# A decoder layer on one core: the first loads of the second stage in another order, and the cast of one bias row moved to an earlier step

## The chip, the core and the metric

The kernel runs on one core of one Trainium2 chip. The metric is the device time of one execution in microseconds (us), as the median of several runs. Five engines work side by side, each through its own list of instructions in order: TensorE (PE, the matmuls), VectorE (DVE), ScalarE (ACT), GpSimd (POOL) and SyncE (SP), which here does nothing but issue transfers (DMAs). ACT issues some transfers as well.

## The reference, cut to what matters

One decoder layer in three blocks, each with a residual and a layer norm behind it; x is 8 x 512 x 512, the context 8 x 512 x 1024, all float32.

```
x1 = layernorm(x  + self_attention(x))            # relative positions, over the axis of 8
x2 = layernorm(x1 + cross_attention(context, x1)) # 8 heads of 64
   # k, v = split(context @ W_src.T + b_src) * mask;  q = (x1 @ W_tgt.T + b_tgt) * mask
   # out  = concat(x1, softmax(q k / 8, masked) v) @ W_out.T + b_out
y  = layernorm(x2 + ffn(x2))
   # h = relu(x2 @ w1.T + b1) rounded to fp8;  w2 rounded to fp8, b2 rounded to fp16
   # ffn = round16(h @ w2.T + b2)
```

## The kernel before, in words

The work falls into two stages. **Stage one** does the self attention for all rows and projects the context of all eight batches to keys (kd) and values (vd), which it stores to device memory together with x1 (x1d). A scheduler orders it. Its last piece is the context of batch 6: `project_context` makes four key tiles (psk, L158) and four value tiles (psv, L172) on TensorE. ScalarE evicts each and issues its store (L167 and L181) right behind the eviction. The context of batch 7 is left for the second stage (the tiles ct7a and ct7b).

**Stage two** does cross attention and feed forward for the batches t = 0 to 7 under a manual schedule: on PE, DVE, ACT and SP the instructions stand in the order in which the Python code emits them. `weave` mixes two lists: the "dense" steps (projections, hidden layer) and the attention steps (`scores`, `attend_next`). `run` executes a step and, ahead of it, spends a credit of 0.7 of the step's cost on the list `side` (softmax work in small pieces, each with a cost) and calls `move`.

The steps that matter around the change, for batch t, head pair c and query half jj:

- `load` (L726) fetches a mask row (mbc). `load_x1T` (L755) fetches x1 of a batch as four transfers into x1Ts, and `turn_x1` (L759) transposes its 32 x 32 blocks on DVE (L753). `queries` (L822) multiplies x1Ts by w_tgt (psq, L825), and DVE evicts to qT (L832).
- `scores` (L836) makes the score tiles s (L845, two in PSUM at a time). DVE takes each out and finds its extreme (pe and nmax, L860), ACT takes the exponential (L870), DVE divides (L885) and transposes blocks into pb (L897).
- `move_blocks` (L902) copies pb to pT in 16 transfers on SP (L910). There is one pT buffer, so the 16 for head pair c can begin only when the `attend` of c - 1 (av, L945) has been done.
- `load_v` (L778) fetches the values of a head pair into the one buffer raw, in four transfers (L788). `turn_v` (L793) transposes them on DVE into vx (L799), and POOL multiplies by the mask (L803). `attend` needs both pT and vx.
- `later` holds loads that are due after some further calls of `move` (a count, taken down by one in each call, run when it falls below zero). `moves` holds the block moves, and in each call of `move` they go ahead of what `later` holds.
- `stage` and `convert` (L1085 and L1090) fetch w2 in four quarters (w2f) and cast each on DVE to fp8 (L1091). `cast_b2` (L1097) fetches the row b2 to all partitions (b2f, L1099) and casts it to fp16 (b2q, L1100). b2f takes one of the seven buffers with the tag "pe" in the pool sp, which the softmax tiles pe and the context tiles kst and vst share.

In the first round (t = 0) the dense steps are six of the eight tiles of batch 7's context (psk, psv) and the queries of batch 1. The dictionary `behind` hangs the casts on these steps by number.

The SP list at the head of the second stage is, in order: w_src (two halves), w_tgt, w_xo, then the output bias row bxo (L93, called from L719), x1Ts in four transfers, w2f, kT twice, raw in four, the next mask row, ct7a and ct7b, x1Ts of batch 1, and x1 of batch 0. In the built program bxo lies where the first context tile of batch 6 was, and so waits for TensorE to have read that tile for the last time.

Each transfer of SP or ACT uses one of eight counters in turn (as the built program lists them), and first waits until the transfer that used this counter before has landed.

Of the kernel before, what the change touches and what calls it, by code (L numbers as in the profile page):

```python
# [9 lines left out]
F32 = mybir.dt.float32  # L10
# [7 lines left out]
P = 128  # L18
E = 512
# [19 lines left out]
R_BQ, R_RW, R_BO, R_BXO, R_B2 = range(5)  # L39
# [3 lines left out]
def decoder_layer(  # L43
# [22 lines left out]
    nc = tc.nc  # L66

    def chunked(w):
        return w.rearrange("(c p) o -> p c o", p=P)
# [21 lines left out]
    def load_row(pool, r, name):  # L91
        tl = pool.tile([P, E], F32, name=name)
        nc.sync.dma_start(tl, rows[r].partition_broadcast(P))  # L93
        return tl
# [92 lines left out]
    with ExitStack() as ph:  # L187
# [439 lines left out]
        t = T - 2  # L627
# [29 lines left out]
    with ExitStack() as ph:  # L657

        def pool(name, bufs, **kw):
            return ph.enter_context(  # L660
                tc.tile_pool(name=name, bufs=bufs, reuse_waits="tile", **kw)
            )

        wb = pool("wb", 1)
# [3 lines left out]
        sp = pool("sp", 7)  # L668
# [10 lines left out]
        urgent, side = [], []  # L679
# [11 lines left out]
        moves, later = [], []  # L691
# [24 lines left out]
        x1Ts = wb.tile([P, 2, EC, S], F32, name="x1Ts")  # L716
        w_xo = wb.tile([P, 2 * EC, E], F32, name="w_xo")
        nc.sync.dma_start(w_xo, chunked(w_xoT))
        bxo = load_row(wb, R_BXO, "bxo")  # L719
        w2q = wb.tile([P, HC, E], F8, name="w2q")  # L720
        b2q = wb.tile([P, E], F16, name="b2q")

# [22 lines left out]
        def load_blocks(dst, src):  # L745
            for a in range(4):
                nc.sync.dma_start(
                    dst[32 * a : 32 * a + 32].rearrange("p c (m e) -> p c m e", e=32),
                    src.rearrange("j (g r) (c a e) -> a r c (j g) e", r=32, a=4, e=32)[a],
                )  # L750

        def turn_in_place(dst, c):
            nc.vector.transpose(dst[:, c], dst[:, c])  # L753

        def load_x1T(t):  # L755
            x1T[t] = x1Ts[:, t % 2]
            load_blocks(x1T[t], x1d[t])

        def turn_x1(t):  # L759
            for c in range(EC):  # L760
                turn_in_place(x1T[t], c)
# [16 lines left out]
        def load_v(p):  # L778
            t, c = p // EC, p % EC
            if p >= T * EC:  # L780
                return
            if t >= T - 2:
                v[t, c] = kvd.tile([P, ST, P], F32, tag="v", name=f"vx{t}_{c}")
                nc.sync.dma_start(v[t, c], vd[t][:, :, c * P : (c + 1) * P])
                return
            raw[p] = kvd.tile([P, 4, P], F32, tag="raw", bufs=1, name=f"raw{p}")
            for g in range(4):
                nc.sync.dma_start(  # L788
                    raw[p][32 * g : 32 * g + 32],
                    vd[t][:, c, g * P : (g + 1) * P].rearrange("(b r) q -> r b q", r=32),  # L790
                )

        def turn_v(p):  # L793

            t, c = p // EC, p % EC
            v[t, c] = kvd.tile([P, ST, P], F32, tag="v", name=f"vx{t}_{c}")
            nc.vector.transpose(  # L799
                v[t, c].rearrange("p s (b e) -> p b s e", e=32),  # L800
                raw[p].rearrange("p b (s e) -> p b s e", e=32),
            )
            nc.gpsimd.tensor_tensor(  # L803
                v[t, c],
                v[t, c],
                maskcol[:, t, :].unsqueeze(2).to_broadcast([P, ST, P]),
                ALU.mult,
            )
            if p + 1 < (T - 2) * EC:
                later.append([2, lambda: load_v(p + 1)])  # L810

        def turn_v_soon(p):
            if p < (T - 2) * EC:
# [271 lines left out]
        def stage(q):  # L1085

            w2f.append(qx.tile([P, HC // 4, E], F32, tag="hq", name=f"w2f{q}"))
            nc.sync.dma_start(w2f[q], chunked(w2T)[:, q * 4 : q * 4 + 4, :])
# [6 lines left out]
                stage(q + 1)  # L1095

        def cast_b2():  # L1097
            b2f = sp.tile([P, E], F32, tag="pe", name="b2f")
            nc.sync.dma_start(b2f, rows[R_B2].partition_broadcast(P))  # L1099
            side.append((("b2", 0), 0.5, lambda: nc.vector.tensor_copy(b2q, b2f)))  # L1100

        def of(cost, f, *a):
            return [(cost, lambda: f(*a))]
# [63 lines left out]
        with tc.manual_schedule(engines={ET.PE, ET.DVE, ET.Activation, ET.SP}):  # L1167
            mq = load(0)
            load_x1T(0)
            stage(0)  # L1170
            for c in range(2):
                load_k(0, c)
            load_v(0)
            turn_x1(0)
            for o in range(EC):
                queries(0, o, mq)
            scores(*units[0])
            turn_v_soon(0)

            for t in range(T):  # L1180
                dense = []
                projected = 0
                mq = load(t + 1) if t + 1 < T else None
                asked = [of(3.6, queries, t + 1, o, mq) for o in range(EC) if t + 1 < T]
                asked = sum(asked, [])
                if t == 0:

                    ct = [
                        qx.tile([P, FC // 2, S], F32, tag="x2T", name="ct7a"),
                        qx.tile([P, FC // 2, S], F32, tag="x1", bufs=2, name="ct7b"),  # L1190
                    ]
                    for i in range(2):
                        nc.sync.dma_start(
                            ct[i],
                            chunked(ctxT[T - 1])[:, i * (FC // 2) : (i + 1) * (FC // 2), :],
                        )
                    load_x1T(1)
                    load_x1(0)
                    pieces = project_context(
                        T - 1,  # L1200
                        w_src[:, :, 0:E],
                        w_src[:, :, E:],
                        lambda f: ct[f // (FC // 2)][:, f % (FC // 2), :],
                        ps_b,
                        "b",
                        sp,
                        "pe",
                    )
                    steps = sum([of(7.2, piece) for piece in pieces[:-2]], []) + asked

                    behind = {
                        1: of(0.0, convert, 0),
                        3: of(0.0, convert, 1),
                        4: of(0.0, turn_x1, 1),
                        5: of(0.0, convert, 2) + of(0.0, cast_b2),
                        7: of(0.0, convert, 3),
                    }
                    for i, step in enumerate(steps):
                        dense += [step] + behind.get(i, [])
                    queried = len(dense)  # L1220
                else:
                    done = [of(3.8, finish, t - 2, j, NJ) for j in range(NJ) if t > 1]
                    if t == 1:

                        done = [of(7.2, pieces[-2]), of(7.2, pieces[-1]), [], []]
                    dense += output_of(t - 1)
                    projected = len(dense)

                    if t + 1 < T:
                        dense += of(0.0, load_x1T, t + 1)  # L1230
                    dense += done[0] + of(0.0, normalize_x2, t - 1)
                    dense += done[1] + of(0.0, load_x2T, t - 1)
                    if t == 1:
                        dense += of(0.0, load_w1)
                    dense += done[2]
                    if t + 1 < T:
                        dense += of(0.0, turn_x1, t + 1)
                    dense += done[3]
                    dense += asked[:2] + of(0.0, turn_x2, t - 1) + asked[2:]
                    queried = len(dense)  # L1240
                    for n in range(HC):
                        dense += of(3.6, hidden, t - 1, n)
                        if n == HC // 4:
                            dense += of(0.0, load_x1, t)
                weave(dense, attention_of(t, projected, queried))

            last = of(3.8, finish, T - 2, 0, NJ) + output_of(T - 1)
            last += of(0.0, normalize_x2, T - 1)
            for j in (1, 2):
                last += of(3.8, finish, T - 2, j, NJ)  # L1250
            for j in range(NJ):
                last += of(0.6, turn_last_x2, j)
            last += of(3.8, finish, T - 2, 3, NJ)
            for n in range(HC):
                last += of(3.6, hidden, T - 1, n)
            for j in range(NJ):
                last += of(3.8, finish, T - 1, j, 1)
            for cost, step in last:
                run(cost, step)
            settle(("y", T - 1))  # L1260
# [88 lines left out]
```

## Time and profile before

| what | value |
|---|---|
| median of 3 runs | 2140.01 us (2139.88 to 2142.92) |
| the profiled execution's own time | 2137.83 us |
| its span in the trace | 2136.0 us |
| busy: PE, DVE, ACT, POOL | 2059.9, 1435.1, 467.5, 172.1 us |
| mean granted TensorE clock | 0.989 |
| PE idle, 890 to 1116 us, by waits | 7.9, 9.0, 0.4, 6.1, 4.5, 1.2 and 0.7 us |

Times in the views are counted from the start of the span. A line of the timeline gives the start, the duration, the engine and line, the operation with the tiles it writes and reads, the number of instructions merged, and in brackets the idle time ahead of it with what ended it. SPq and ACTq are the transfers issued by these engines; their duration is that of issuing, not of the transfer. The table of windows gives the busy time of each engine in each stretch, with the granted TensorE clock (1.00 is full).

### The profile page before, as it was taken

Reading aid. Unit: us, or ns where it says so; the run is one execution under the profiler, and the core shown is the slowest. Engines: PE = TensorE matmul, PEld = TensorE weight load, DVE = VectorE, ACT = ScalarE, POOL = GpSimd, SP = SyncE. Lnnn points to the kernel's source line nnn. Section 1 sums busy time; section 2 is a strip of 40 time slices with the busy share of each in tenths; the row PEclk is TensorE's granted clock in tenths of the full one; section 3 lists DMA queues with packets and bytes.
Section 4 is the critical chain, followed back from the end, with each engine's and each line's share of the span. In section 5 each row is a group of like instructions: output and inputs, shape, how many; then the busy total and the mean of one; then the engine's idle time right before and its main releaser. Section 6 shows DMA issues by size and latency. Waiting matters only on the chain.

```text
span 2136.0 us, 17269 instructions
## 1 busy us (share of the span) xinstructions
PE 2059.9 (96%) x5768; PEld 881.0 (41%) x5768; DVE 1435.1 (67%) x2285; ACT 467.5 (22%) x955; POOL 172.1 (8%) x147
## 2 busy tenths in 40 slices
PE   9899999999999999897999999999999999999998
PEld 5444444444444444342334443444444434443443
DVE  4999999999999994076454664845747648356332
ACT  3011102101200111122133232332332332323211
POOL 0201010110012010010101011010010100000000
PEclk9999999999999999998899999999999999999999
DMA  6511430454015355675484653745647538436200
GB/s 213 202 44 44 183 114 20 153 190 166 13 55 202 118 187 179 157 186 133 99 204 117 111 136 78 140 109 98 133 100 113 133 85 148 101 72 150 57 20 20
DMA packets 246201, 255.27 MB, mean 120 GB/s; under 512 B 141024, under 2 KB 161504, under 8 KB 246112
## 3 DMA queue, kind: packets, MB, share of 16 engines
q1 hardware_dynamic: 228736, 223.45, 41.3%
q10 hardware_dynamic: 17376, 30.71, 4.0%
q8 instruction: 46, 0.75, 0.1%
q14 instruction: 43, 0.35, 0.1%
HBM read 130.36 MB, written 56.62 MB: 88 GB/s over the span
## 4 chain that ended last, share of the span: by engine, by line
PE 67%; DVE 22%; DMA 5%; issue 3%; SPq 2%; POOL 1%; ACT 1%; ACTq 0%; DVEq 0%; POOLq 0%
PE h L1037 20%; PE pox L982 5%; PE av L945 5%; PE s L845 5%; PE psq L825 5%; PE pox L970 5%; PE o L1054 4%; DVE pq L388 4%; DVE sc L397 4%; DVE pv L437 4%; PE px L553 3%; DVE pv L447 2%; PE psk L158 2%; PE ps_q L212 2%; PE psv L172 2%
## 5 line engine op out<-in xcount | busy, mean ns | idle before, releaser
L1037 PE MATMUL h<-x2T,w 128*128 128x512 f32 x1024 | 454.2, 599 | 4.8 <-DVE x2T L753 4.8
L1037 PEld LDWEIGHTS h<-x2T,w 128*128 128x128 f32 x1024 | 192.0, 191 | 263.4 <-issue 255.6
L860 DVE CUSTOM_DVE_ANT_0 pe<-s,mb 128x512 f32<-128x512 f32 x256 | 162.1, 681 | 204.4 <-PE s L845 204.4
L870 ACT ACTIVATE pe<-pe,nmax 128x512 f32<-128x512 f32 x256 | 182.2, 712 | 234.0 <-DVE nmax L860 231.7
L897 DVE STREAM_TRANSPOSE pb<-pe 128x512 f32<-128x512 f32 x256 | 159.6, 679 | 0.0
L1044 ACT ACTIVATE hq<-h,colv 128x512 fp8e4<-128x512 f32 x128 | 88.0, 687 | 294.3 <-PE h L1037 294.3
L437 DVE TENSOR_TENSOR pv<-v,sc 128x2048 f32<-128x2048 f32 x64 | 149.6, 2338 | 2.0
L388 DVE TENSOR_TENSOR pq<-qw,k 128x2048 f32<-128x2048 f32 x64 | 148.3, 2317 | 1.2
L397 DVE TENSOR_REDUCE sc<-pq 128x64 f32<-128x2048 f32 x64 | 146.0, 2281 | 1.3
L845 PE MATMUL s<-kT,qTx 64*128 64x512 f32 x512 | 129.5, 623 | 9.5 <-DVE nmax L860 9.4
L945 PE MATMUL av<-pT,vx 128*64 128x512 f32 x512 | 121.6, 619 | 11.3 <-DMA pT<-pb 6.1
L212 PE MATMUL ps_q<-w_in,xt 128*128 128x512 f32 x256 | 119.7, 597 | 6.3 <-DVE qw L374 6.3
L825 PE MATMUL psq<-x1Ts,w_tgt 128*128 128x512 f32 x256 | 115.4, 603 | 9.1 <-DVE x1Ts L753 9.1
L212 PE MATMUL ps_k<-w_in,xt 128*128 128x512 f32 x256 | 115.5, 601 | 5.3 <-DMA xt<-in_xT_dram 4.9
L463 PE MATMUL po<-w_o,aoT 128*128 128x512 f32 x256 | 119.1, 608 | 0.7 <-ACT aoT L460 0.7
L885 DVE TENSOR_SCALAR pe<-pe,rden 128x512 f32<-128x512 f32 x256 | 116.4, 497 | 4.5
L982 PE MATMUL pox<-w_xo,uT 128*128 128x512 f32 x256 | 115.2, 598 | 0.0
L970 PE MATMUL pox<-w_xo,x1Ts 128*128 128x512 f32 x256 | 114.4, 595 | 0.0
L1054 PE MATMUL o<-w2q,hq 128*128 128x512 fp8e4 x512 | 114.1, 379 | 0.0
L212 PE MATMUL ps_v<-w_in,xt 128*128 128x512 f32 x256 | 112.0, 594 | 0.0
L473 POOL TENSOR_TENSOR r<-r,bo 128x512 f32<-128x512 f32 x32 | 55.6, 1763 | 507.5 <-DMA r<-in_x_dram 438.8
L989 DVE TENSOR_TENSOR x<-pox,x 128x512 f32<-128x512 f32 x32 | 22.1, 692 | 104.7 <-PE pox L982 66.7
(142 smaller groups left out, 2163.2 us busy)
## 6 DMA issues: line engine op xcount, KB each, us to landing
pT<-pb SPq DMA_DIRECT2D x512, 128.0 KB, 2.4
ch<-in_ctxT_dram SPq DMA_DIRECT2D x24, 512.0 KB, 5.9
td<-tx SPq DMA_DIRECT2D x12, 768.0 KB, 5.9
tx<-td SPq DMA_DIRECT2D x12, 768.0 KB, 7.9
r<-in_x_dram SPq DMA_DIRECT2D x32, 256.0 KB, 3.6
x1d<-r ACTq DMA_DIRECT2D x32, 256.0 KB, 2.5
x1Ts<-x1d SPq DMA_DIRECT2D x32, 256.0 KB, 6.2
kT<-kd SPq DMA_DIRECT2D x32, 256.0 KB, 3.2
```

The costliest lines, as they stand in the source:

```text
L212: nc.tensor.matmul(ps, lhsT=xt[:, e, :], rhs=w_in[:, e, part * E : (part + 1) * E], start=(e == 0), stop=(e == EC - 1),)
L388: nc.vector.tensor_tensor(pr, qw[:, fs] .rearrange("p (h d) -> p h d", d=D1) .unsqueeze(2) .to_broadcast([P, HH, T, D1]), k_all[:, :, fs]. ...
L397: nc.vector.tensor_reduce(sc[:, t, g * HH * T : (g + 1) * HH * T], pr.rearrange("p h s d -> p (h s) d"), AX.X, ALU.add,)
L437: nc.vector.tensor_tensor(pr, v_all[:, :, fs].rearrange("p s (h d) -> p s h d", d=D1), sc[:, t, g * HH * T : (g + 1) * HH * T] .rearrange( ...
L825: nc.tensor.matmul(ps, lhsT=w_tgt[:, e, o * P : (o + 1) * P], rhs=x1T[t][:, e, :], start=(e == 0), stop=(e == EC - 1),)
L845: nc.tensor.matmul(ps[:, h, :], lhsT=qT[t][half[h], c, j * P : (j + 1) * P], rhs=kT[t, c][half[h], :], start=True, stop=True,)
L870: nc.scalar.activation(pe, pe, AF.Exp, bias=nmax[:, h : h + 1], scale=-1.0, accum_out=den[:, h : h + 1],)
L945: nc.tensor.matmul(av[half[h], :], lhsT=v[t, c][:, s, half[h]], rhs=pT[t, c][:, :, :, s, h].rearrange("p g i q -> p (g i) q"), start=(s == 0),
L970: nc.tensor.matmul(po, lhsT=x1T[t][:, e, j * P : (j + 1) * P], rhs=w_xo[:, e, :], start=(e == 0), stop=False,)
L982: nc.tensor.matmul(po, lhsT=uT[t][:, e, j * P : (j + 1) * P], rhs=w_xo[:, EC + e, :], start=False, stop=(e == EC - 1),)
L1037: nc.tensor.matmul(ps, lhsT=w1[0][:, e, n * P : (n + 1) * P], rhs=x2T[t][:, e, :], start=(e == 0), stop=(e == EC - 1),)
L1054: nc.tensor.matmul(po, lhsT=hq[t][:, c, j * P : (j + 1) * P], rhs=w2q[:, c, :], start=(c == 0), stop=(c == HC - 1),)
```

## The change

Four edits, all of which act in the first round of the second stage:

- The load of bxo is issued behind the four transfers of x1Ts for batch 0 instead of ahead of them.
- The load of b2f is issued behind the first raw load, with the first loads of the stage, instead of behind the third quarter of w2.
- The cast to b2q stands behind the first quarter's cast, as a step of its own, instead of in the list `side` behind the third quarter.
- In batch 0 the load of the next raw is due in the next call of `move` (count 0) instead of two calls later (count 2).

```diff
@@ ahead of the stage
         nc.sync.dma_start(w_xo, chunked(w_xoT))
-        bxo = load_row(wb, R_BXO, "bxo")
         w2q = wb.tile([P, HC, E], F8, name="w2q")
@@ turn_v(p)
             if p + 1 < (T - 2) * EC:
-                later.append([2, lambda: load_v(p + 1)])
+                later.append([2 if t else 0, lambda: load_v(p + 1)])
@@ cast_b2()
         def cast_b2():
-            b2f = sp.tile([P, E], F32, tag="pe", name="b2f")
-            nc.sync.dma_start(b2f, rows[R_B2].partition_broadcast(P))
-            side.append((("b2", 0), 0.5, lambda: nc.vector.tensor_copy(b2q, b2f)))
+            nc.vector.tensor_copy(b2q, b2f)
@@ the manual schedule
             load_x1T(0)
+            bxo = load_row(wb, R_BXO, "bxo")
             stage(0)
             for c in range(2):
                 load_k(0, c)
             load_v(0)
+            b2f = sp.tile([P, E], F32, tag="pe", name="b2f")
+            nc.sync.dma_start(b2f, rows[R_B2].partition_broadcast(P))
@@ behind, t == 0
-                        1: of(0.0, convert, 0),
+                        1: of(0.0, convert, 0) + of(0.0, cast_b2),
...
-                        5: of(0.0, convert, 2) + of(0.0, cast_b2),
+                        5: of(0.0, convert, 2),
```

## The prediction

> **What bounds the kernel now.** I read the page's part 1 and its slices first, then the waits of TensorE between 820 and 1120 us, then, for each long wait, the chain and the timelines of SP and DVE around it. PE is busy for 96% of the span and idle in few places. So a change pays only where it closes an idle stretch of PE, or the slow clock behind one.
>
> ```profile
> PE 2059.9 (96%) x5768; PEld 881.0 (41%) x5768; DVE 1435.1 (67%) x2285; ACT 467.5 (22%) x955; POOL 172.1 (8%) x147
> PEclk9999999999999999998899999999999999999999
> ```
>
> The clock dips in two slices alone, from about 960 to 1070 us. The waits of PE around there (total, times, longest):
>
> ```profile
> PE s L845 <- DVE nmax L860: 9.4, 2, 9.0
> PE psq L825 <- DVE x1Ts L753: 9.1, 2, 7.9
> PE av L945 <- DMA pT<-pb: 6.1, 1, 6.1
> PE av L945 <- POOL vx L803: 4.5, 1, 4.5
> ```
>
> Four stalls; behind them PE runs until 1936 us with under 2 us of waiting. The chain shows what feeds three of them. At the head of the stage:
>
> ```profile
> 864.01 21.47 PE psv L172 x50
> ...
> 885.50 0.34 SPq L93
> ...
> 891.69 6.83 DMA x1Ts<-x1d
> ...
> 898.64 0.72 DVE x1Ts L753
> ```
>
> SP stood at bxo (L93) until TensorE had read the first context tile for the last time. x1Ts was queued behind it, and its last piece landed at 898.5. PE ran out at 891.47 and went on at 899.41. In the middle:
>
> ```profile
> 983.56 5.66 DMA b2f<-in_rows_dram
> ...
> 989.24 0.43 DVE b2q L1100
> 989.67 0.60 DVE pe L860
> ...
> 990.95 3.79 PE s L845 x8
> ```
>
> DVE stood at the cast of b2 until its row landed, with the score evictions (L860) queued behind it. PE, done at 981.94, waited for these until 990.95. And at the end of the round, on SP:
>
> ```profile
> 1020.07 11.30 SPq L910 DMA_DIRECT2D pT<-pb  x16
> 1031.47 1.95 SPq L788 DMA_DIRECT2D raw<-vd  x4
> ```
>
> The values of the last head pair go out behind 16 moves. They land at 1035.1, are turned and masked, and av starts at 1037.19 where PE was free at 1032.65.
>
> **Part 1: x1 ahead of bxo.** Nothing is added; five transfers change places on SP. In the built program's list of waits the four x1Ts pieces now wait for the landing of four ACT stores alone, two of keys and two of values (issued at 857.90, 864.76, 871.63 and 878.50; such stores land in 2.4 us, one in 6.9). So the last piece goes out at about 881. Issue (0.7) and landing (4.3, the least of the x1Ts rows, to 6.8, the row above) bring it to 886 to 888.5, and the first turn (0.72) to 889.2 at the latest. That is 2.3 us before PE ends psv. The stall of 7.94 goes.
>
> What is passed: bxo waits for a later context tile and goes out at about 888.8. w2f keeps its own wait for the last psv (891.47) and kT its wait for the last value store (894.7 by the row), so these move by 2 us or less. bxo's reader, POOL at 925, keeps over 20 us of cover.
>
> The clock behind the stall: the four psq groups took 15.46 us (899.41 to the first s at 914.87). Two groups at full clock take 7.07 (1083.54 to 1090.61), so four take 14.14; 1.3 was lost. Sum: 7.94 + 1.3 = **9.2**, less whatever is late next. That is ct7a, needed at 891.47 + 14.14 + 1.95 (scores) = 907.6, and ct7b 3.5 later. Before they landed at 910.6 and 913.8 (issued 905.01 and 905.63, landing 5.6 and 8.2). They stood behind w2f, which shared the transfers with 1 MB of x1Ts and took 11.3 us; the other three w2f took 5.4 to 6.4. With x1Ts out of the way w2f lands at about 897.5 and kT at 899. ct7a goes out at about 900, with four raw and two row transfers ahead of it on SP, and lands at 905.6. Bounds of the wait: 0 (this reckoning) to 3.0 (ct7 no earlier than before). I take 0.
>
> **Part 2: b2.** One transfer moves ahead of the mask row (0.35 us of SP, behind raw). One cast of 0.43 us moves on DVE to behind the first w2 cast, where DVE has a wait of 4.07 us for ACT a little later: nothing. In the old place DVE leaves the turn of the values at 982.65 + 0.70 = 983.35 and starts L860 there, not at 989.59: **6.2** earlier. PE's stall shrinks from 9.0 to 2.8; the rest is PE's own last psq, its eviction, the turn and the first L860. What is late next on DVE: the cast of w2's last quarter follows these four L860, and w2f is issued behind 16 moves as before, so DVE will wait for it some 3 us. Behind it stand divides and the eviction of the next psq, for which DVE has waits of 3.17 and 2.25 us on PE now, so this costs PE nothing. b2f holds one of seven buffers for longer. The list of waits shows one new wait from that: ACT's eviction kst (941.92) needs the first kst's store (issued at 924.68), which has 17.2 us for a landing of 2.4 to 6.9.
>
> The clock is the open size. The 2.8 us that stay have a nearest row, a gap of 2.88 us in stage one (columns as in the table of windows; PE busy first, clock third from the right):
>
> ```profile
> 608.96:612.37 3.41, 1.18 (x5) 0.48 (x5) 3.41 (x5) 0.59 (x1) 3.30 (x3) 1.00 0.00 0
> 612.37:615.78 3.41, 3.41 (x5) 1.51 (x5) 3.41 (x3) 0.00 (x0) 0.00 (x0) 0.50 0.00 0
> 981.01:984.43 3.42, 0.93 (x3) 0.10 (x1) 1.37 (x2) 0.00 (x0) 1.00 (x1) 1.00 0.89 200
> ```
>
> Eight matmuls took 5.39 us behind it, against 3.6 elsewhere. So the clock can still fall to a half. Before, the score pair behind the stall took 3.71 (990.95 to 994.66) against 1.92, of which 0.35 is its second L860: 1.4 to 1.5 lost, which I leave lost, by that row. [...]
>
> **Part 3: raw ahead of the moves.** raw is one buffer, free once DVE has turned the pair before. That turn is at 1011.28, well ahead of the moves at 1020.07, and SP has nothing else from 1012.7 to 1020.07. So the four issues (1.95 us) fit there. The first raw load of the round moves ahead of a w2f as well, issued 23 us ahead of its cast. What is late next for av: the moves. The last is issued at 1030.77 (or 1029.5 at the 10.03 us that the three other sets take), lands 2.38 later, and av starts 0.46 behind that: 1032.3 to 1033.6, against PE free at 1032.65. The stall falls from 4.54 to between 0 and 1.0: 3.6 to 4.5, I take 4.0. With no gap the slow clock goes too: av took 6.19 (to 1043.38) against 3.59 elsewhere (969.11 to 972.70), 2.6. Sum **6.6**.
>
> Not touched: the 6.1 us before the third av. It is the way from one av through 16 issues (10.03) and a landing (2.38) to the next, and it keeps its clock loss.
>
> **Sum**: 9.2 + 6.2 + 6.6 = 22.0. The span goes from 2136.0 to 2114.0, the profiled execution's own 2137.83 to 2115.8. The runs' median is 2.2 above that execution, so on its scale 2140.0 - 22.0 = **2118.0**. All that follows from 1037 on moves as a block, since PE sets its time.
>
> **Rivals.**
> - *The clock is kept behind the short gap.* Depends on where 2.8 us fall against the stretches of 3.4. Gives 1.5 more: 2116.5. Chance 0.20.
> - *The head's gain is partly given back.* ct7a and ct7b land when they did; PE waits 3.0 and loses 1.5 to 1.9 by clock: 2122.7. For it: the windows show DMA at 0.8 to 1.4 of its engines from 886 to 904. Against: the 1 MB of x1Ts is then gone from that stretch. 0.13.
> - *Part 3 gives nothing*, since the moves are stretched (one set took 11.30, one 15.45): 2118.0 + 6.6 = 2124.6. 0.06.
> - *x1 does not come earlier*, if its last piece had to wait for the last value store as kT does: it lands at about 900, and 9.2 is lost: 2127.2. Against: the list names the store before that. 0.03.
> - *Slower*: the buffer that b2f holds. ACT takes its work in order; if the first kst store lands later than 17.2 us after its issue, the exponentials behind that eviction, DVE's divides and the moves wait, one for one. To eat 22.0 and 4.3 more it needs 43.5 us. The longest such store is 6.9, so I give it 0.03.
> - *No change* (within 0.2%), if another wait that I do not see takes each place: 0.03.
>
> **How the numbers follow.** The forecast has 0.52. Faster by over 0.2% (4.3 us, about what a measurement of this kernel can tell from no change) are the forecast and four rivals: 0.94. Within: 0.03. Slower: 0.03. The range: at the low end all bounds at once, 9.2 + 7.7 + 7.1 = 24.0, on the profiled execution's own scale 2113.8, less a little; at the high end the case of part 3: 2113.0 to 2125.0. Left out are 0.09 and the tails.
>
> **What would show it.** The first psq right behind psv with no wait on x1Ts; else step 1 is wrong, and the wait names the piece. No idle time on DVE ahead of b2q, PE's wait for nmax at 2.8, and a new DVE wait of about 3 us at the fourth w2 cast. raw ahead of the moves on SP, and the fourth av waiting 1 us or less, for pT. The third av still waits 6.1. A wait of psk for ct7a or ct7b would be the second rival. A change in the stretches from 1120 on would make the whole reckoning wrong.

## The result, and the profile after

The changed kernel takes 2117.76 us (median of 4 runs, 2116.41 to 2119.34), the kernel before 2141.47 beside it; the ratio is 0.9897, with a 95% interval of 0.9885 to 0.9909. Forecast were 2118.0 and a range of 2113 to 2125. Over all runs of the study the change has a mean of 2118.9 (17 runs) and the kernel before, as it ran beside the others, 2140.8 (31 runs): 21.9 us less, where the sum of the steps was 22.0. The steps do not all agree as well as that sum, as the trace shows.

The profiled execution took 2119.34 us, its span 2117.6. The page, with the granted clock of TensorE in 40 slices:

```profile
PE 2058.4 (97%) x5768; PEld 881.4 (42%) x5768; DVE 1434.4 (68%) x2285; ACT 467.4 (22%) x955; POOL 173.3 (8%) x147
PEclk9999999999999999999999999999999999999999
```

PE has as much to do as before, in a span that is 18.4 us shorter, and the dip of the clock is gone from the slices (each covers 53 us; shorter stretches at half clock remain, such as 3.4 us from 911.82 and 6.8 from 1000.57). The waits of PE between 820 and 1120 us (total, times, longest):

```profile
PE av L944 <- DMA raw<-vd: 6.3, 2, 5.6
PE s L844 <- DVE nmax L859: 3.4, 2, 2.7
PE psk L158 <- DMA ct7a<-in_ctxT_dram: 3.0, 1, 3.0
PE psq L824 <- DVE x1Ts L752: 1.7, 1, 1.7
```

Two of the four stalls are gone, one has shrunk from 9.0 to 2.7, one stays, and one is new: psk for ct7a. (The 1.7 us for x1Ts are those of batch 1, 1.2 before, and lie later.) The first queries of the stage and the waits that matter stand in PE's timeline:

```profile
892.66 13.90 PE L824 MATMUL psq<-x1Ts,w_tgt 128*128 128x512 f32 x32
...
911.50 5.40 PE L158 MATMUL psk<-ct7a,w_src 128*128 128x512 f32 x8 [3.03 <-DMA ct7a<-in_ctxT_dram]
...
981.00 2.35 PE L844 MATMUL s<-kT,qTx 64*128 64x512 f32 x8 [2.66 <-DVE nmax L859]
...
1002.89 5.87 PE L944 MATMUL av<-pT,vx 128*64 128x512 f32 x16 [5.63 <-DMA raw<-vd]
...
1021.30 3.65 PE L944 MATMUL av<-pT,vx 128*64 128x512 f32 x16
```

The first psq has no bracket: it follows the last psv (its end at 892.82 overlaps the start by a little) without a wait. The fourth av has none either, and takes 3.65 us. Before, it read:

```profile
1037.19 6.25 PE L945 MATMUL av<-pT,vx 128*64 128x512 f32 x16 [4.54 <-POOL vx L803]
```

The third av's bracket names raw, but that can't be what av waited for: the raw load issued at 1001.08 is for the next pair and landed at 1003.05, behind the start of av. Its values were ready at 1002.24 (POOL), and the last move into pT landed at 1002.43, 0.46 ahead of av. So it still waits for the moves, as before.

The chain of waits tells why psk waited:

```profile
865.35 27.48 PE psv L172 x64
892.86 0.69 ACT vst L180
893.58 5.96 DMA vd<-vst
...
903.30 8.15 DMA ct7a<-in_ctxT_dram
911.50 8.83 PE psk L158 x16
```

The last store of values took 5.96 us to land. kT, which waits for that store's counter, was issued at 899.60. Behind it stood the second kT, raw, b2f and the mask row; ct7a went out at 903.30 and took 8.15.

The two executions do not have the same stage one: its last psv ends at 891.47 before and 892.82 after. So stage two is compared from there to the end of the span: 1244.5 us before, 1224.8 after, **19.7** less. Where these come from, by differences of the two timelines, up to the end of the fourth av:

| place | forecast | measured | how |
|---|---|---|---|
| head: stall and clock of psq | -9.2 | -9.6 | 7.94, and psq to the first s 15.46 against 13.82 |
| head: ct7a | 0 | +4.7 | wait 3.03, and 8.76 for the psk of ct7a and ct7b, 7.07 where the clock stays (ct7 ahead, below) |
| b2: stall | -6.2 | -6.3 | 9.00 to 2.66 |
| b2: clock behind it | 0 | -1.4 | the s pair 3.71 against 2.28 |
| next wait for nmax | 0 | +0.4 | 0.39 to 0.75 |
| third av | 0 | -0.4 | 6.11 to 5.63, and av itself 5.71 to 5.80 |
| fourth av | -6.6 | -7.2 | 4.54 to 0, and 6.19 against 3.58 |
| sum | -22.0 | -19.8 | |

From the fourth av on all moves as a block: PE's place differs by 18.5 us there and by 18.4 at the end.

### The profile page after: what moved, and what is told of

It is laid out like the page before. It is cut to its first block, busy times and chain, and to the rows that moved or that the text cites. A ratio compares the mean times of both kernels' runs of the same rounds, so it can differ in the third digit from the quotient of the medians.

```text
span 2117.6 us, 17267 instructions
## 1 busy us (share of the span) xinstructions
PE 2058.4 (97%) x5768; PEld 881.4 (42%) x5768; DVE 1434.4 (68%) x2285; ACT 467.4 (22%) x955; POOL 173.3 (8%) x147
## 4 chain that ended last, share of the span: by engine, by line
PE 69%; DVE 22%; DMA 5%; issue 2%; SPq 1%; ACT 1%; POOL 0%; ACTq 0%; DVEq 0%; POOLq 0%
PE h L1036 21%; PE pox L981 5%; PE pox L969 5%; PE s L844 5%; PE av L944 5%; PE o L1053 4%; PE px L553 4%; PE psq L824 4%; DVE pq L388 4%; DVE sc L397 4%; DVE pv L437 4%; DVE pv L447 2%; PE psk L158 2%; PE psv L172 2%; PE ps_q L212 2%
```

## Experiments

Each kernel's time stands beside runs of the kernel before on the same chip. "Stage two" is the stretch from the end of the last psv to the end of the span in the kernel's profile.

**One part at a time.** Three kernels, each the kernel before with one part of the change.

The first has the move of bxo alone:

```diff
-        bxo = load_row(wb, R_BXO, "bxo")
...
             load_x1T(0)
+            bxo = load_row(wb, R_BXO, "bxo")
```

> The kernel before with the first edit alone: bxo behind the four x1Ts transfers. The reckoning on record: PE no longer waits for x1Ts (7.9) and loses no clock there (1.3), 9.2 us less. Theory drawn from the profile after: w2f now goes out while the last value store of batch 6 is under way, that store lands late (5.96 us there, against 2.4), kT waits for it and ct7a is queued behind kT, so psk waits about 3 us for ct7a and loses 1.8 by clock: 4.4 us less in all, PE's wait for ct7a 3 us, the store at about 6 us. Rival: the ct7a wait belongs to the b2 row, which stands ahead of ct7a on SP only in the whole change; then no ct7a wait here and 9 us less. The stalls for b2 (9.0) and for raw (4.5) stay as they were in all cases.

The second has b2's load and cast alone (the edits to `cast_b2`, its load behind `load_v(0)`, and `behind`, as in the change):

> The kernel before with the b2 row loaded behind raw and cast behind the first quarter, and nothing else. Reckoning on record: PE's wait for nmax goes from 9.0 to 2.8 us, 6.2 us less, and 1.5 more if the granted clock stays full behind the short gap (in the profile after it did): 6.2 to 7.7 us less. Rival: the moves set the time of the round and the next av gives the gain back, 0 to 2 us less. The stall at the head stays at 7.9.

The third has the count of the raw load alone:

```diff
-                later.append([2, lambda: load_v(p + 1)])
+                later.append([2 if t else 0, lambda: load_v(p + 1)])
```

> The kernel before with the third part alone: the next raw load due at once in batch 0. Reckoning on record: the wait of the fourth av falls from 4.5 to between 0 and 1 us, and its slow clock (2.6) goes: 6.6 us less, at most 7.1. Rival: the moves are the later of the two and the wait only changes its name from values to moves, 0 to 2 us less. The stalls at the head (7.9) and for b2 (9.0) stay.

| kernel | median | ratio to before (95%) | stage two less by |
|---|---|---|---|
| x1 alone | 2132.55 | 0.9962 (0.9949 to 0.9975) | 5.8 |
| b2 alone | 2130.98 | 0.9949 (0.9936 to 0.9962) | 6.5 |
| raw alone | 2133.79 | 0.9964 (0.9951 to 0.9978) | 6.2 |

The waits of PE between 820 and 1120 us (total, times, longest), with x1 alone:

```profile
PE s L844 <- DVE nmax L859: 10.2, 2, 9.8
...
PE av L944 <- POOL vx L802: 4.1, 1, 4.1
PE psk L158 <- DMA ct7a<-in_ctxT_dram: 2.3, 1, 2.3
```

The same view with b2 alone:

```profile
PE psq L825 <- DVE x1Ts L753: 9.8, 2, 7.9
...
PE s L845 <- DVE nmax L860: 3.1, 2, 2.7
```

And with raw alone:

```profile
PE s L845 <- DVE nmax L860: 10.4, 2, 10.0
PE psq L825 <- DVE x1Ts L753: 9.1, 2, 8.0
...
PE av L945 <- issue: 0.5, 1, 0.5
```

Each part takes away its own stall and leaves the others (with raw alone, 0.5 us is left of the fourth av's 4.5). The three gains in stage two add up to 18.5 against 19.7 for the whole, so in the profiles the parts hardly help or hinder each other. The runs are too coarse to say it: their medians are 8.9, 10.4 and 7.6 us below the kernel before, 26.9 together against 23.7 for the whole beside its own, and each has a 95% interval of about 2.8 us to either side. With x1 alone 4.4 us were expected; 5.8 by the profile and 8.9 by the runs is more. The wait of psk for ct7a is there with x1 alone, without b2's row ahead of it: it belongs to part 1. With b2 alone the clock did fall behind the short gap (at half from 985.7 to 989.1); in the changed kernel's first profile it did not.

**w2 behind the values.** The changed kernel, with the first w2f issued behind raw and b2f:

```diff
-            stage(0)
             for c in range(2):
                 load_k(0, c)
             load_v(0)
             b2f = sp.tile([P, E], F32, tag="pe", name="b2f")
             nc.sync.dma_start(b2f, rows[R_B2].partition_broadcast(P))
+            stage(0)
```

> The changed kernel with the first quarter of w2 issued behind kT, raw and the b2 row instead of ahead of kT. Theory that w2f's 1 MB beside the last value store delays that store and, through kT's wait, ct7a: the store lands in 2.4 to 3 us, the list behind it moves up by 3 us, psk waits under 1 us for ct7a and keeps its clock: 4 to 5 us less than the changed kernel, 28 less than before, 2113. Rival: it is the sum of the bytes that makes ct7a late, whatever their order: the wait of about 3 us stays and the time is that of the changed kernel, 2118. A second rival: w2f then shares its time with ct7a itself, and about half is gained.

It took 2117.94 (ratio 0.9891, 0.9876 to 0.9905), the same as the changed kernel. From its chain:

```profile
895.28 2.34 DMA vd<-vst
...
901.43 10.50 DMA ct7a<-in_ctxT_dram
```

The last store of values and ct7a, each with its landing. The first link is confirmed: with w2f out of the way the last store lands in 2.34 us. But then w2f is issued at 900.44, right ahead of ct7a, which takes 10.50 instead of 8.15, and psk still waits 1.80. One delay was traded for another. At psk over half was gained, much as the second rival said, for the clock stayed there (1.8 us lost against 4.7). In this execution it fell behind the short gap for nmax instead, and stage two took 1223.6. The 4 to 5 us of the expectation did not come.

How w2f holds the store up can be seen in the DMA queues of the changed kernel's first profile. From 893.40 to 897.80, and from 897.80 to 899.00 (packets, MB, share of the 16 DMA engines):

```profile
q1 hardware_dynamic: 479, 0.98, 72.2%
...
q10 hardware_dynamic: 144, 0.26, 57.4%
q1 hardware_dynamic: 49, 0.07, 15.2%
```

q1 carries SP's transfers, here w2f, and q10 ACT's, here the store. The store was issued at 893.58, but in the first stretch not one packet of it moved. Its first packet starts at 897.84, and all 0.26 MB have moved by 898.95. So in this profile the store's data did not move beside those of w2f: they came when 479 packets, 0.98 MB, had moved on q1. With w2f out of the way its first packet starts 0.8 us after the issue.

**ct7 ahead of w2.** So both loads of the context were put ahead of w2f, b2f and the mask row, and taken out of their old place at the head of the first round:

```diff
-            stage(0)
             for c in range(2):
                 load_k(0, c)
             load_v(0)
+            ct = [ ... ct7a, ct7b ... ]
+            for i in range(2):
+                nc.sync.dma_start(ct[i], ...)
+            stage(0)
             b2f = sp.tile([P, E], F32, tag="pe", name="b2f")
```

> The changed kernel with ct7a and ct7b issued ahead of the first w2f, of b2f and of the mask row. Theory (the second rival as traced: the 4.8 us that psk loses after the change, 3.0 of waiting and 1.8 of clock, come from w2f's 1 MB, which delays the last value store from 2.4 to 5.96 us and with it kT, raw and ct7a on SP, or shares the transfers with ct7a): with w2f issued last, the last value store lands in about 2.4 us, kT goes out at about 896, ct7a a little behind raw at about 899 to 900 and lands in 5.6 to 6, by about 906; psk waits for nothing and each of its groups takes 3.5 us. From the end of psv to the end of the span 4 to 4.8 us less than the 1224.8 of the changed kernel, so 1220 to 1221, and a median some 4.5 less than that kernel's. Rival (ct7a is late for another reason, such as the four raw and two kT transfers ahead of it, or the sharing with them): psk waits 1.5 to 3 us as in the changed kernel and with w2f behind raw, and the time is the same within 0.1%. A cost to look for: w2f lands 5 to 8 us later than after the change (900), so its cast, and the cast of b2 behind it on DVE, could stand in the way of an eviction; if w2f lands only by 915, DVE waits at its first cast and the scores behind it lose up to some 5 us, which would eat the gain.

SP's timeline in its first profile:

```profile
895.95 1.85 SPq L787 DMA_DIRECT2D raw<-vd  x4
897.90 0.40 SPq L1176 DMA_DIRECT2D ct7a<-in_ctxT_dram  x1
898.34 0.51 SPq L1176 DMA_DIRECT2D ct7b<-in_ctxT_dram  x1
898.89 0.51 SPq L1087 DMA_DIRECT2D w2f<-in_w2T_dram  x1
```

And in PE's timeline, the first psk:

```profile
908.05 3.70 PE L158 MATMUL psk<-ct7a,w_src 128*128 128x512 f32 x8
```

No bracket: ct7a, out at 897.90 and landed in 5.7, is there before PE asks for it at 908.05, and the clock stays. Stage two took 1220.6. w2f was the later one, landing in 10.1, and DVE's first cast, at 918.74, did not wait for it. The four times (2114.86 to 2122.12) did not settle the size, so this kernel and the changed one ran twice more:

> The kernel with ct7a and ct7b ahead of w2f once more, to settle its size. In its first profile psk waited for nothing and the stretch from psv to the end took 1220.6 us against 1224.8 and 1223.9 of the changed kernel; its four times (2114.9 to 2122.1) do not tell it from that kernel's. Theory (the 4.8 us at psk are gained for good): psk again without a wait, 1220 to 1222 from psv to the end, and over all its runs a mean 3 to 4.5 us below that of the changed kernel. Rival (the gain is given back elsewhere, or lies within what the executions differ by): means within 1.5 us of each other, and the profile shows where.

> The changed kernel beside it: psk waits 2 to 4 us for ct7a, 1223 to 1226 from psv to the end. The clock falls behind a gap or not by where the gap lies against windows of 3.41 us whose place is another in each execution: a window in which PE is busy for under 1.5 us is followed by one at half clock, one of over 1.8 us is not. So the gap of 2.7 us at the nmax costs 1.4 to 1.7 more in some executions than in others.

> A third profile and more runs, for the mean: as before, no wait of psk, and 1220 to 1222 from psv to the end. Whether the clock falls behind the gap of 2.7 us at the nmax follows from the windows: a gap that leaves under 1.5 us of work in one window of 3.41 halves the next one.

> A third profile and more runs of the changed kernel, for the mean: psk waits 2 to 4 us, and 1223 to 1226 from psv to the end, by whether the clock falls behind the gap at the nmax.

Together with one more run of the changed kernel (expectation under the clock, below):

| kernel | stage two, by profile | mean of the runs |
|---|---|---|
| changed | 1224.8, 1223.9, 1225.5, 1223.4 | 2118.9 (17 runs) |
| ct7 ahead | 1220.6, 1220.6, 1219.8 | 2116.4 (12 runs) |

In the profiles the gain is 4.1 us and the two groups do not touch. In the runs it is 2.5, with a 95% interval of about 0.6 to 4.4 (standard errors 0.64 and 0.68); beside each other on the same chip the means differ by 2.1 and by 3.3. The 3 to 4.5 expected for the means were thus not reached, though the interval holds them. This version beats both kernels, by an amount that the runs alone give only roughly.

The 4.1 of the profiles are not psk alone. In the four profiles of the changed kernel psk lost 4.7, 4.3, 4.8 and 2.4 by wait and clock, 4.1 on average. Some 0.6 more come from the gap at the nmax, behind which the clock fell in two of those four profiles and in none of these three; that goes by where the grid described below lies, and not by the order of the loads. About as much is given back at the fourth av, which here waits 0.31 to 0.85.

**The cast in its old place.** The changed kernel with b2's row loaded early, but cast where it was:

```diff
-            nc.vector.tensor_copy(b2q, b2f)
+            side.append((("b2", 0), 0.5, lambda: nc.vector.tensor_copy(b2q, b2f)))
...
-                        1: of(0.0, convert, 0) + of(0.0, cast_b2),
+                        1: of(0.0, convert, 0),
...
-                        5: of(0.0, convert, 2),
+                        5: of(0.0, convert, 2) + of(0.0, cast_b2),
```

> The changed kernel with b2's row loaded early as there, but its cast left in its old place, in the list of small softmax pieces behind the third quarter of w2. Theory (the wait was for the row's landing alone): the row has long landed, the cast costs DVE 0.43 us in that place and nothing else; PE's wait for nmax is 2.7 to 3.1 us against 2.66, and the time is that of the changed kernel within 0.5 us, plus up to 1.5 us if the clock falls behind the slightly longer gap. Rival (the place of the cast matters, because it stands between evictions that PE waits for): the wait grows by more than the 0.43 us of the cast, and the time by 2 us or more.

2119.66, beside 2119.27 for the changed kernel in the same set. PE's wait:

```profile
981.24 2.82 PE L844 MATMUL s<-kT,qTx 64*128 64x512 f32 x8 [3.00 <-DVE nmax L859]
```

3.00 against 2.67, less than the cast's own 0.43. So the stall was the landing of the row; the place of the cast is worth a third of a microsecond. Its profile is that of the slowest of its four runs (2122.60), and stage two took 1228.4 there, some 4 more than in the changed kernel: PE ran at half clock for five windows of 3.41 us between 900 and 1020, against three or four there, and psk waited 3.58.

**The changed kernel again, and the one before again.**

> The changed kernel once more, beside the other two on the same chip. As in its own runs: about 2118, 0.989 to 0.991 of the kernel before; from the end of psv to the end of the span 1224 to 1226; psk waits 2 to 3 us for ct7a; the s behind nmax waits 2.7, with or without a slow stretch of 1.5 us behind it, by where the gap falls against the clock's windows.

> The kernel before once more, for a second profile. The first profiled execution took 2137.8, about 3.6 less than the 2141.4 that its runs have as a median elsewhere. Theory (the executions differ in stage one, whose end lay anywhere from 890.8 to 894.5 in the kernels tried, which share that stage): from the end of psv to the end of the span it takes 1244.5 again within 1.5 us, and what differs lies ahead of that. Rival (the second stage of the first profile was a lucky one): from psv to the end 1247 or more, and then the change gained more in the second stage than the 19.7 of the first pair of profiles.

The changed kernel: 2119.27, stage two 1223.9, psk waiting 2.87. The kernel before: 2138.79, stage two 1245.7, which is within the 1.5 us expected. By four and two profiles, stage two went from 1245.1 to 1224.4, so 20.7 less.

**Why the clock falls behind the same gap in one execution and not in another.** The runs of one kernel answer this. In each profile every edge of a stretch at half clock (between 560 and 1125 us) lies on one grid of 3.413 us, and the grid lies elsewhere in each execution. Two profiles of the changed kernel, the first one and the last repeat, have the same grid. The table of windows of the first (PE busy first, granted clock third from the right):

```profile
976.67:980.09 3.42, 1.67 (x4) 0.38 (x2) 2.08 (x4) 0.00 (x0) 0.27 (x1) 1.00 0.97 213
980.09:983.50 3.41, 2.40 (x9) 0.82 (x10) 2.08 (x8) 2.93 (x8) 0.78 (x1) 1.00 0.89 253
```

And of the last repeat:

```profile
976.67:980.09 3.42, 0.76 (x4) 0.08 (x2) 2.71 (x7) 0.71 (x2) 1.04 (x1) 1.00 0.95 192
980.09:983.50 3.41, 3.41 (x8) 1.02 (x8) 1.09 (x4) 2.22 (x8) 0.00 (x0) 0.50 0.96 321
```

The gap is 2.66 and 2.67 us long. In the first it starts at 978.34 and is cut in two by the edge at 980.09: PE is busy for 1.67 of 3.42, and the clock stays. In the second it starts at 977.34 and lies in one window: 0.76 busy, and the next window runs at half clock; the s pair takes 3.61 us up to the next psq, where it took 2.28. Over the fourteen profiles, every window at full clock with PE busy for 1.36 us or less (40%) was followed by half clock, and none with 1.67 or more (49%). Between these lie twelve windows, of which four were. One of the other eight has 1.43 us (at 908.41 in the last repeat), so the bound of 1.5 us in the expectations does not hold in all fourteen. The gap of 2.7 to 3.0 us lost the clock in five of ten profiles.

## Why the prediction was right, and where its steps were not

**Part 1** was right in what it takes away: psq follows psv without a wait, and 9.6 us go where 9.2 were forecast. The step that failed is the one that set ct7a's wait to 0, "ct7a goes out at about 900, with four raw and two row transfers ahead of it on SP, and lands at 905.6". It went out at 903.30 and landed at 911.45. Since psv ended 1.35 us later than in the profile before, this is 2.0 and 4.5 us behind the forecast.

Two terms were wrong. The first is the landing of the last value store, for which kT waits. It was put at 2.4 ("894.7 by the row"), as other stores took with nothing large beside them; it took 5.96, so kT went out at 899.60, and the eight transfers ahead of ct7a (two kT, four raw, two rows) took SP 3.7 us more. The warning stood in the profile before: there the same store took 4.43, beside the megabyte of x1Ts. The change took x1Ts out of its way and put w2f there. The second is the landing of ct7a, taken as the 5.6 of before; it was 8.15. It landed 3.1 us behind the mask row, the transfer ahead of it on SP, where before it had landed 2.9 behind it. So its landing goes with that of the transfer ahead of it, here as before, and the 5.6 was not a time of its own. (That the other three w2f took 5.4 to 6.4 is also misread: they took 5.4, 5.6 and 7.2.)

The stall that the second rival named came true: its 3.0 of waiting and 1.5 to 1.9 of clock were 3.03 and 1.69. Its time, 2122.7, did not. That its 3.0 fits is in part luck, since it rests on ct7a landing at 910.6; in the second profile of the kernel before ct7a landed at 907.90. It had been given 0.13 because x1Ts' megabyte was gone from the stretch; it was not x1Ts that held ct7a up, but the store behind w2f, and then the queue on SP. The first link is shown by w2 behind alone; ct7 ahead removes both at once, and with them the whole wait.

**Part 2** was right in its mechanism and in 6.2 (measured 6.3, and 2.66 for what stays against 2.8). The price of the clock was taken from one row of stage one. It is no fixed price: 1.1 to 1.7 us are lost, in half of the profiles. By an estimate from the table above, the clock is kept behind a gap of 2.7 when no window gets more than about 1.8 of it, and an edge in the right 0.9 us of 3.41 does that: about one time in four. Kept it was in five of ten. The first rival (0.20) was thus not another course of the kernel, but a matter of each execution. The half clock did not need a window without work: in the last repeat 0.76 us of it in the window from 976.67 did not prevent it. The new wait of DVE at the fourth w2 cast is there, at 4.56 us against some 3 forecast, and costs PE 0.4 at the next nmax in this profile; in the two profiles of the changed kernel in which the clock fell, PE comes later and waits 0.39 there, as before.

**Part 3**: 7.2 against 6.6. The fourth av waits for nothing, the better end of 0 to 1.0. "Not touched" held for the third av: from the end of one av to the start of the next 12.4 us before (1001.88 to 1014.26) and 12.4 after (990.50 to 1002.89). The wait is put down to raw or to vx in some profiles and to pT in others, but the last move landed behind the values in three profiles: by 0.7 before, and by 0.2 and 0.7 in the first profile of the changed kernel and its last repeat. So by this estimate a faster way for the moves alone would give some 0.2 to 0.7 there before the values set the time; it was not tried.

**The slower rival** (b2f's buffer, and a late store of kst) did not show: there is no wait of PE behind it.

**The sum** of 22.0 stands against 19.7 in the first pair of profiles, 20.7 over six, and 21.9 in the runs' means; by the medians beside each other it is 23.7. The median agrees with the forecast to 0.3 us, which is luck: the steps deserve no better than 2 to 3 us. Of the loss of 4.7 at ct7a, 2.5 is made up by the rest: 0.4 at the head, 1.4 of clock, 0.6 at the fourth av, 0.1 at the three small rows. Then comes the scale: the runs of the kernel before lie at 2140.8 on average, while its two profiled executions took 2137.8 and 2138.8. The longer ones have the lower mean clock: of 27 runs with the clock on record, the nine at 0.988 took 2141.5 on average and the three at 0.991 took 2138.1. Where in the execution they lost it cannot be seen, since they have no trace.

**Open.** Stage one ended at 890.8 to 891.6 in the four profiles with bxo in its old place and at 891.6 to 895.7 (mean 893.5) in the ten with bxo behind x1Ts. The instructions up to there stand in the same order on every engine but for bxo on SP, and psv takes 27.63 in all of them. The granted clock shows where the time went: up to there the four have one window of 3.41 us at half clock each, the ten have two to four, and the end moves with their number (with two 891.6 to 894.5, with four 894.2 to 895.7). Six of the ten have the first of them at 38 and 79 us, over 800 us ahead of the load that was moved, so its place cannot act on these directly. Why none of the four has as many, chance or not, stays open; if it is a cost of the change, it is some 2 us.

## What to carry to other kernels

When a transfer is moved away, ask what moves into its place, and which landing the next transfers wait for: here a store that 1 MB of x1Ts had delayed to 4.43 us was delayed to 5.96 by the 1 MB of w2f, and the list behind it waited for that. Then write down the issue time of everything behind it on the queue, one by one, and count a load's landing from that of the transfer ahead of it (2.5 to 3.8 us behind it for 1 MB here). What is needed first goes out first: both context loads put ahead of w2f gave 4.1 us of stage two in the profiles, where moving w2f alone gave some 1. And a short stall's clock loss is a chance, not a price: lay the gap against the window of 3.41 us that the profiles show here, in all its places, before putting a number on it.

## What the runs showed of the hardware

- The last store of values landed in 2.3 us with no w2f near it (four profiles), in 4.4 to 4.8 beside 1 MB of x1Ts (the four with bxo in its old place) and in 5.7 to 6.0 with w2f issued 0.7 us ahead on another engine's queue (six). In the six it landed 0.8 to 0.9 us behind w2f, and in the first profile of the changed kernel none of its packets moved in the first 4.2 us after the issue: its data themselves began to move only at 897.84.
- ct7a, 1 MB, landed 5.6 to 10.5 us after its issue, but 2.5 to 3.8 us behind the transfer issued just ahead of it on SP in all fourteen profiles. With raw ahead of it there (ct7 ahead) it took 5.7, with w2f and the mask row (w2 behind) 10.5.
